# Order and grain of the W1 loads and weight sums beside a masked first layer

## The chip, the cores and the metric

The kernel runs on one core of one Trainium2 chip. The metric is the device time of one execution in microseconds (us), given as the median of several runs. "The profile" is one execution recorded by the hardware profiler; all lines L... are lines of the kernel before unless said otherwise.

## The reference

Eight batches of x (256 rows, 1024 features, float32) go through two residual layers:

```python
sign = (2 * mask - 1).astype(x.dtype)            # one 1024 x 1024 mask per batch
x = x + (einsum('bsi,oi->bso', x, W0) + b0 + einsum('bsi,bio->bso', x, sign) * coeff[:, None, None])
A, Bm = lora_As[itok], lora_Bs[itok]             # rank 16, one of 32 slots per batch
x = x + (einsum('bti,oi->bto', x, W1) + b1 + 2.0 * einsum('btr,bro->bto', einsum('bti,bir->btr', x, A), Bm))
```

In the first layer every batch has a weight matrix of its own, W0 + coeff * (2*mask - 1). In the second all batches share W1, and a small low-rank product is added.

## The kernel before

**First layer.** Work is cut into 64 pieces, numbered k: 8 batches b, two halves h of 512 output features, four groups g of 256 input features (two chunks c of 128). `load(k)` issues on SyncE's queue (SP) the transfers of a piece: the mask block `m` (512 KB), for batch 0 also the block of W0 (512 KB, kept for all batches), for h = 0 the block of x (256 KB). `build(k)` makes the weights: ScalarE (ACT) turns the mask into plus or minus coeff (L188), and VectorE (DVE) adds W0 (L191). TensorE (PE) multiplies in `first_layer` (L215): 8 float32 matmuls a piece, which the trace shows as 16 records. After four pieces VectorE evicts the result with bias and residual into `y` (L229, four instructions). Loads run four pieces ahead of the matmuls in the program and builds two ahead. Masks and built weights have three buffers each (`mpool`, `wpool`): mask k can be loaded only after ScalarE has read mask k-3, and weights k can be built only after TensorE has finished piece k-3.

**Grain.** For k < NG (= 4) the mask and W0 are loaded, and the weights built, by single chunks (two transfers of 256 KB, two ACT and two DVE instructions of 512 columns); from k = 4 on by whole blocks (`chunks`, `load`, `by_chunk`). `by_chunk` reorders the arrays on the host side so that one chunk lies in one stretch of memory.

**Second layer.** Four batches form a group, and there are two groups (pieces 0 to 31 and 32 to 63). After its pieces, `second_layer` multiplies by W1 with a Winograd-Strassen scheme on two levels: seven outer products (A11, A12, S1, S2, S4, S3, A22), each with seven inner leaves (a11, s1, s2, a12, s3, a22, s4). The left leaves are sums of blocks of W1. They are made once, beside the first layer of group 0, by the generator `combine_weights`: W1's 16 blocks (256 KB each, `raw[q, r]`) are loaded, the identity is added on the diagonal (L260), and VectorE forms inner sums (L269 to L275) and outer sums (L286). GpSimd (POOL) writes each leaf to a DRAM scratch (`keep`, L245), from which SyncE loads it when needed (`load_leaves`, L361). The inner sums take their buffers from a pool of seven (`lpool`), which a leaf's write frees.

**Where the W1 loads and the sums stand.** In `load`, each of batch 1's pieces (k = 8 to 15) is followed by two blocks of W1, row by row of the matrix (L176 to L180). `step`, called after each piece as `beside`, takes three items of the sums' generator; the generator is started ahead of b = 1, h = 1, so from k = 12 on. It adds the identity to all four diagonal blocks first and then makes A11, A12, A22, S1, S2, S4, S3. A list scheduler in the framework places the instructions of each engine in order; `tc.issue_after(i)` holds what is under it behind instruction i in that order. [...]

Of the kernel before, what the change touches and what calls it, by code (L numbers as in the profile page):

```python
# [13 lines left out]
P = 128  # L14
OH = 512
CG = 2
OQ = 256
SCALING = 2.0


@with_exitstack
def kernel(
# [36 lines left out]
    nc = tc.nc  # L59
    B, NG, _, _, T = xT.shape  # L60
# [67 lines left out]
    ident = const.tile([P, P], F32, tag="ident", name="ident")  # L128
# [3 lines left out]
    x_sb, m_sb, weff, w0_sb, raw, weff_at = {}, {}, {}, {}, {}, {}  # L132
    pieces = [(b, h, g) for b in range(B) for h in range(2) for g in range(NG)]

    def quad(name):
        return qpool.tile([P, CG, OQ], F32, tag="q", name=name)

    def chunks(k: int):

        return [slice(c, c + 1) for c in range(CG)] if k < NG else [slice(0, CG)]  # L140

    def chunk(a, c: int):

        flat = a.rearrange("p c f -> (p c f)")
        return flat.rearrange("(c p f) -> c p f", c=CG, p=P)[c]

    def load(k: int):


        b, h, g = pieces[k]  # L150
        m_sb[k] = mpool.tile([P, CG, OH], I32, tag="m", name=f"m_{k}")
        if b == 0:
            w0_sb[h, g] = const.tile([P, CG, OH], F32, tag=f"w0{h}{g}", name=f"w0_{h}_{g}")
        if h == 0:
            x_sb[b, g] = xpool.tile([P, CG, T], F32, tag=f"x{g}", name=f"x_{b}_{g}")
        pairs = [(m_sb[k], mask[b, h, g])]
        if b == 0:
            pairs.append((w0_sb[h, g], w0T[h, g]))
        if h == 0:
            pairs.append((x_sb[b, g], xT[b, g]))  # L160
        if k < NG:

            for c in range(CG):
                for i, (t, a) in enumerate(pairs):
                    if i < 2 or k == 0:
                        nc.sync.dma_start(t[:, c], chunk(a, c))  # L166
                    elif c == 0:
                        nc.sync.dma_start(t, a)
        else:
            for t, a in pairs:  # L170
                nc.sync.dma_start(t, a)  # L171
        if k == NG:
            nc.sync.dma_start(b0_sb, b0)
        if k == 2 * NG:
            nc.sync.dma_start(itok_sb, itok)
        if b == 1:  # L176
            n = h * NG + g
            for q, r in ((n // 2, 2 * (n % 2)), (n // 2, 2 * (n % 2) + 1)):
                raw[q, r] = quad(f"w1_{q}_{r}")
                nc.sync.dma_start(raw[q, r], w1T[q, r])  # L180

    def build(k: int):
# [12 lines left out]
    BUILDS_AHEAD = 2  # L195
    n_pieces = len(pieces)
# [4 lines left out]
    def first_layer(b: int, h: int, y, beside):  # L201


        ps = [bank(f"ps1_{b}_{h}_{i}") for i in range(TPH // 2)]
        for g in range(NG):
            k = (b * 2 + h) * NG + g
            if k + LOADS_AHEAD < n_pieces:
                load(k + LOADS_AHEAD)
            if k + BUILDS_AHEAD < n_pieces:
                build(k + BUILDS_AHEAD)  # L210
            w = weff.pop(k)
            for c in range(CG):
                for j in range(TPH):
                    first = g == 0 and c == 0
                    nc.tensor.matmul(  # L215
                        ps[j // 2][:, j % 2, :],
                        lhsT=w[:, c, j * P : (j + 1) * P],
                        rhs=x_sb[b, g][:, c, :],

                        start=first and j % 2 == 0,  # L220
                        stop=g == NG - 1 and c == CG - 1,
                        skip_group_check=True,
                    )
            beside()

        with tc.issue_after(weff_at[k + BUILDS_AHEAD].ins) if b == 0 else nullcontext():
            for j in range(TPH):
                ot = h * TPH + j
                nc.vector.scalar_tensor_tensor(  # L229
                    y[:, j, :],  # L230
                    ps[j // 2][:, j % 2, :],
                    b0_sb[:, ot : ot + 1],
                    x_sb[b, ot // CG][:, ot % CG, :],
                    ALU.add,
                    ALU.add,
                )
# [4 lines left out]
    def keep(outer, inner, t):  # L241
        leaf_at[outer, inner] = dram.tile(
            [P, CG, OQ], F32, tag=f"{outer}{inner}", name=f"leaf_{outer}_{inner}"
        )
        nc.gpsimd.dma_start(leaf_at[outer, inner], t)  # L245

    def combine_weights():


        quads = {  # L250
            f"A{i + 1}{j + 1}": {
                (u, v): raw[2 * i + u, 2 * j + v] for u in range(2) for v in range(2)
            }
            for i in range(2)
            for j in range(2)
        }
        for q in range(NG):
            for c in range(CG):
                d = raw[q, q][:, c, c * P : (c + 1) * P]
                nc.vector.tensor_add(d, d, ident)  # L260
                yield

        def inner(name, blocks, own):
            a11, a12, a21, a22 = (blocks[u, v] for u in range(2) for v in range(2))
            s = {}
            for n in ("s1", "s2", "s3", "s4"):
                s[n] = lpool.tile([P, CG, OQ], F32, tag="l", name=f"{name}_{n}")
                if n == "s1":
                    nc.vector.tensor_add(s[n], a21, a22)  # L269
                elif n == "s2":  # L270
                    nc.vector.tensor_sub(s[n], s["s1"], a11)
                elif n == "s3":
                    nc.vector.tensor_sub(s[n], a11, a21)
                else:
                    nc.vector.tensor_sub(s[n], a12, s["s2"])  # L275
                keep(name, n, s[n])
                yield
            for n, t in (("a11", a11), ("a12", a12), ("a22", a22)):
                if n in own:
                    keep(name, n, t)  # L280

        def outer(name, op, x, y):
            tiles = [tpool.tile([P, 2, CG, OQ], F32, tag="T", name=f"{name}_{u}") for u in range(2)]
            out = {(u, v): tiles[u][:, v] for u in range(2) for v in range(2)}
            for uv in out:
                op(out[uv], x[uv], y[uv])  # L286
                yield
            quads[name] = out

        for i, j, name in ((0, 0, "A11"), (0, 1, "A12"), (1, 1, "A22")):  # L290
            for n, (u, v) in (("a11", (0, 0)), ("a12", (0, 1)), ("a22", (1, 1))):
                leaf_at[name, n] = w1T[2 * i + u, 2 * j + v]
        every = ("a11", "a12", "a22")
        yield from inner("A11", quads["A11"], ("a11", "a22"))
        yield from inner("A12", quads["A12"], ())
        yield from inner("A22", quads["A22"], ("a11", "a22"))
        yield from outer("S1", nc.vector.tensor_add, quads["A21"], quads["A22"])
        yield from inner("S1", quads["S1"], every)
        yield from outer("S2", nc.vector.tensor_sub, quads["S1"], quads["A11"])
        yield from inner("S2", quads["S2"], every)  # L300
        yield from outer("S4", nc.vector.tensor_sub, quads["A12"], quads["S2"])
        yield from inner("S4", quads["S4"], every)
        yield from outer("S3", nc.vector.tensor_sub, quads["A11"], quads["A21"])
        yield from inner("S3", quads["S3"], every)
# [274 lines left out]

    sums = iter(())  # L580

    def step():
        for _ in range(3):
            next(sums, None)

    for group in range(NGROUP):
        if group:
            load_adapters(group)
        y = [
            [  # L590
                ypool.tile([P, TPH, T], F32, tag=f"y{i}{h}", name=f"y_{GB * group + i}_{h}")
                for h in range(2)
            ]
            for i in range(GB)
        ]
        first = Right(f"b11_{group}", [y[0][0], y[1][0]])
        second = Right(f"b21_{group}", [y[0][1], y[1][1]])
        for i in range(GB):
            for h in range(2):
                if i == 1 and h == 1 and group == 0:  # L600
                    sums = combine_weights()
                if i == 3:
                    for _ in (first, second)[h].sums():
                        pass
                first_layer(GB * group + i, h, y[i][h], step)
                if group == 0 and i == 2 and h == 0:
                    late = y[i][h][:, 0, :1]
                    begin_adapters(late)
                    load_adapters(group, late)
        for _ in sums:  # L610
            pass
        second_layer(group, y, first, second)
# [69 lines left out]
```

## Time and profile before

| | us |
|---|---|
| median of 3 runs (lowest to highest) | 424.54 (424.22 to 425.1) |
| the profiled execution | 424.1 |
| its span, first to last instruction | 422.2 |
| TensorE busy in the span | 414.3 (98%) |
| VectorE busy | 271.4 (64%) |
| TensorE's first L215 matmul | 5.83 |
| last stall of TensorE ahead of L215 ends | 61.82 |
| second layer of group 0 begins | 120.80 |

The chain of work that ended last is TensorE alone from 61.82 us to 418.7 us, except for the eviction and the store at the very end. Stretches are given in us from the span's start. A matmul record is drawn with a duration of about 380 ns, but records overlap: TensorE issues one each 216 ns (3.45 us for the 16 records of a piece), so that a stall is read from the distance of starts and not from the busy time.

### The profile page before, as it was taken

To read this page: it belongs to the slowest core of one execution; us is meant where nothing else is said; L and a number is where in the kernel's file an instruction comes from. 1 tells how busy PE (TensorE), PEld (TensorE's weight loads), DVE (VectorE), ACT (ScalarE), POOL (GpSimd) and SP (SyncE) were. 2 spreads that over 40 slices of the span, in tenths; PEclk is the share of its full clock that TensorE was granted. 3 is DMA by queue.
4 is the path that set the end of the run, shared out by engine and by line. 5 is a ranking of instruction groups with operands and counts; after the bars stand their busy time and mean duration, and the time that the engine had idled before them with its cause. 6 is when DMAs were issued, how large, how long until landed. Compare 5 with 4: busy or idle time off the path is not lost.

```text
span 422.2 us, 5655 instructions
## 1 busy us (share of the span) xinstructions
PE 414.3 (98%) x2074; PEld 354.5 (84%) x2074; DVE 271.4 (64%) x395; ACT 110.9 (26%) x126; POOL 38.5 (9%) x77
## 2 busy tenths in 40 slices
PE   8999989999999999999999999999999999999996
PEld 6788868888877888878888888888888688888885
DVE  2457879999765558865735437754573465786693
ACT  4443234333334211011013333333330330101100
POOL 0002313664200000003000000000000000000000
PEclk9999999999999999999999999999999999999999
DMA  8999999999994475557864655744410346654663
GB/s 277 397 404 398 413 408 379 409 336 351 413 395 160 130 254 164 150 174 226 261 222 154 204 201 175 221 152 150 151 50 0 99 108 199 217 153 150 201 205 118
DMA packets 42046, 97.38 MB, mean 231 GB/s; under 512 B 5540, under 2 KB 6308, under 8 KB 42020
## 3 DMA queue, kind: packets, MB, share of 16 engines
q1 hardware_dynamic: 33122, 76.30, 53.7%
q0 software_dynamic: 4288, 12.61, 7.9%
q10 hardware_dynamic: 4610, 8.13, 5.0%
q8 instruction: 16, 0.26, 0.3%
q14 instruction: 10, 0.08, 0.0%
HBM read 77.09 MB, written 19.92 MB: 230 GB/s over the span
## 4 chain that ended last, share of the span: by engine, by line
PE 85%; DMA 12%; SPq 1%; DVE 1%; ACT 0%; issue 0%; DVEq 0%; ACTq 0%
PE ps L215 40%; PE X L378 23%; PE Z L378 12%; DMA w<-w1T 7%; PE Y L378 6%; DMA x<-xT 3%; DMA m<-mask 3%; PE G L395 2%; PE psh L410 2%; SPq L166 1%; ACT w L188 0%; DVE w L191 0%; SPq L171 0%; DVE S L286 0%; DVE c L431 0%
## 5 line engine op out<-in xcount | busy, mean ns | idle before, releaser
L215 PE MATMUL ps<-x,w 128*128 128x256 f32 x1024 | 222.7, 380 | 2.9 <-DVE w L191 2.8
L215 PEld LDWEIGHTS ps<-x,w 128*128 128x128 f32 x1024 | 194.4, 190 | 31.2 <-DVE w L191 4.8
L191 DVE TENSOR_TENSOR w<-w,w 128x1024 f32<-128x1024 f32 (+1 forms) x68 | 78.8, 1159 | 72.5 <-ACT w L188 71.3
L188 ACT ACTIVATE w<-m,neg_c,two_c 128x1024 f32<-128x1024 int32 (+1 forms) x68 | 81.0, 1191 | 163.6 <-PE ps L215 84.2
L512 DVE TENSOR_TENSOR c<-c,e 128x512 f32<-128x512 f32 x48 | 32.0, 687 | 11.2 <-ACT c L404 10.7
L229 DVE SCALAR_TENSOR_TENSOR y<-ps,b_sb,x 128x256 f32<-128x256 f32 x64 | 27.2, 477 | 7.6 <-PE ps L215 7.0
L404 ACT COPY c<-G 128x512 f32<-128x512 f32 x32 | 16.4, 600 | 53.7 <-PE G L395 53.7
L431 DVE TENSOR_TENSOR c<-X,c 128x512 f32<-128x512 f32 (+1 forms) x26 | 16.7, 647 | 16.1 <-PE X L378 16.1
L429 ACT COPY e<-X 128x512 f32<-128x512 f32 x16 | 9.4, 587 | 58.2 <-PE X L378 51.9
L378 PE MATMUL X<-T_t,l_S_s 128*128 128x256 f32 x96 | 22.7, 379 | 0.0
L378 PEld LDWEIGHTS X<-T_t,l_S_s 128*128 128x128 f32 x96 | 18.2, 190 | 2.5
L378 PE MATMUL X<-b_t,l_A_s 128*128 128x256 f32 x64 | 15.5, 386 | 0.0
L431 DVE TENSOR_TENSOR e<-X,e 128x512 f32<-128x512 f32 x16 | 11.0, 686 | 5.8 <-PE X L378 5.8
L378 PEld LDWEIGHTS X<-b_t,l_A_s 128*128 128x128 f32 x64 | 11.8, 190 | 3.0 <-issue 1.5
L431 DVE TENSOR_TENSOR e<-Z,e 128x512 f32<-128x512 f32 x16 | 11.0, 687 | 1.0 <-PE Z L378 0.8
L378 PE MATMUL X<-T,l_S_a 128*128 128x256 f32 x48 | 11.3, 379 | 0.0
L378 PE MATMUL Z<-T_t,l_S_s 128*128 128x256 f32 x48 | 11.3, 379 | 0.0
L378 PE MATMUL Y<-T,l_S_a 128*128 128x256 f32 x48 | 11.3, 379 | 0.0
L378 PE MATMUL X<-T_t,l_S_a 128*128 128x256 f32 x48 | 11.3, 379 | 0.0
L378 PE MATMUL Z<-T,l_S_s 128*128 128x256 f32 x48 | 11.3, 379 | 0.0
L431 DVE TENSOR_TENSOR e<-Y,e 128x512 f32<-128x512 f32 x8 | 5.5, 691 | 7.4 <-PE Y L378 7.4
L378 PEld LDWEIGHTS Y<-T,l_S_a 128*128 128x128 f32 x48 | 9.1, 190 | 1.2
(97 smaller groups left out, 380.0 us busy)
## 6 DMA issues: line engine op xcount, KB each, us to landing
m<-mask SPq DMA_DIRECT2D x60, 512.0 KB, 5.7
l_S_s<-leaf_S_s SPq DMA_DIRECT2D x32, 256.0 KB, 2.7
x<-xT SPq DMA_DIRECT2D x31, 256.0 KB, 6.6
outT<-c ACTq DMA_DIRECT2D x30, 256.0 KB, 3.2
l_A_s<-leaf_A_s SPq DMA_DIRECT2D x24, 256.0 KB, 3.9
l_S_a<-leaf_S_a SPq DMA_DIRECT2D x24, 256.0 KB, 2.6
w<-w1T SPq DMA_DIRECT2D x16, 256.0 KB, 7.6
leaf_S_s<-S_s POOLq DMA_DIRECT2D x16, 256.0 KB, 7.1
```

The costliest lines, as they stand in the source:

```text
L166: nc.sync.dma_start(t[:, c], chunk(a, c))
L188: nc.scalar.activation(w[:, c], m[:, c], AF.Identity, bias=neg_c[:, b : b + 1], scale=two_c[:, b : b + 1])
L191: weff_at[k] = nc.vector.tensor_add(w[:, c], w[:, c], w0_sb[h, g][:, c])
L215: nc.tensor.matmul(ps[j // 2][:, j % 2, :], lhsT=w[:, c, j * P : (j + 1) * P], rhs=x_sb[b, g][:, c, :],  start=first and j % 2 == 0, stop= ...
L229: nc.vector.scalar_tensor_tensor(y[:, j, :], ps[j // 2][:, j % 2, :], b0_sb[:, ot : ot + 1], x_sb[b, ot // CG][:, ot % CG, :], ALU.add, AL ...
L378: nc.tensor.matmul(ps[:, j, :], lhsT=l[:, c, j * P : (j + 1) * P], rhs=r[:, c, :], start=first and c == 0 and j == 0, stop=False, skip_gro ...
L395: nc.tensor.matmul(ps[b][:, j, :], lhsT=lb_pad[rows, o : o + P], rhs=h_sb[rows, :], start=j == 0, stop=j == 1, skip_group_check=True,)
L404: nc.scalar.copy(dest[b // 2][u, b % 2], ps[b])
L410: nc.tensor.matmul(ph[i * S : i * S + R, 0, :], lhsT=a[:, i, c, :], rhs=y[i][c // TPH][:, c % TPH, :], start=(c == 0), stop=(c == NC - 1),)
L429: nc.scalar.copy(out, ps)
L431: nc.vector.tensor_add(out, ps, other)
L512: nc.vector.tensor_add(o, o, x)
```

## The change

Three things change. `BY_CHUNK = 6` takes the place of NG in `chunks`, `load` and `by_chunk`: the six blocks k = 0 to 5 of batch 0 are loaded and built by single chunks, instead of four. The 16 blocks of W1 are loaded in the order A11, A12, A22, A21 (the order in which the sums use them), block n behind the transfers of piece k = 10 + 3n // 4, so one or two a piece over k = 10 to 21, instead of two a piece over k = 8 to 15. The sums start after piece 11, three items a piece up to piece 17 and four from 18 on, and each portion is held behind the weight build of piece k + 2; the identity is added to A11's and A22's diagonal blocks just ahead of their own sums.

```diff
+BY_CHUNK = 6
...
-        return [slice(c, c + 1) for c in range(CG)] if k < NG else [slice(0, CG)]
+        return [slice(c, c + 1) for c in range(CG)] if k < BY_CHUNK else [slice(0, CG)]
...
+    W1_ORDER = [
+        (2 * i + u, 2 * j + v)
+        for i, j in ((0, 0), (0, 1), (1, 1), (1, 0))
+        for u in range(2)
+        for v in range(2)
+    ]
...
-        if k < NG:
+        if k < BY_CHUNK:
 
             for c in range(CG):
                 for i, (t, a) in enumerate(pairs):
...
-        if b == 1:
-            n = h * NG + g
-            for q, r in ((n // 2, 2 * (n % 2)), (n // 2, 2 * (n % 2) + 1)):
+        for n, (q, r) in enumerate(W1_ORDER):
+            if k == 0:
                 raw[q, r] = quad(f"w1_{q}_{r}")
+            if k == 2 * NG + 2 + 3 * n // 4:
                 nc.sync.dma_start(raw[q, r], w1T[q, r])
...
-            beside()
+            beside(k)
...
-        for q in range(NG):
-            for c in range(CG):
-                d = raw[q, q][:, c, c * P : (c + 1) * P]
-                nc.vector.tensor_add(d, d, ident)
-                yield
+
+        def add_identity(blocks):
+            for u in range(2):
+                for c in range(CG):
+                    d = blocks[u, u][:, c, c * P : (c + 1) * P]
+                    nc.vector.tensor_add(d, d, ident)
+                    yield
...
+        yield from add_identity(quads["A11"])
         yield from inner("A11", quads["A11"], ("a11", "a22"))
         yield from inner("A12", quads["A12"], ())
+        yield from add_identity(quads["A22"])
         yield from inner("A22", quads["A22"], ("a11", "a22"))
...
-    def step():
-        for _ in range(3):
-            next(sums, None)
+    def step(k: int):
+
+        nonlocal sums
+        if k == 2 * NG + 3:
+            sums = combine_weights()
+        with tc.issue_after(weff_at[min(k + BUILDS_AHEAD, n_pieces - 1)].ins):
+            for _ in range(3 if k < 4 * NG + 2 else 4):
+                next(sums, None)
...
-                if i == 1 and h == 1 and group == 0:
-                    sums = combine_weights()
...
-    by_chunk(arrays["mask"][0, 0])
-    by_chunk(arrays["w0T"][0])
+    for k in range(BY_CHUNK):
+        by_chunk(arrays["mask"][0, k // NG, k % NG])
+        by_chunk(arrays["w0T"][k // NG, k % NG])
```

## The prediction

> **What bounds the kernel now.** I read the page's busy line and DMA slices first, then who kept TensorE waiting, then the chain of work, then the timeline at the stalls.
>
> ```profile
> PE 414.3 (98%) x2074; PEld 354.5 (84%) x2074; DVE 271.4 (64%) x395; ACT 110.9 (26%) x126; POOL 38.5 (9%) x77
> DMA  8999999999994475557864655744410346654663
> ```
>
> TensorE bounds the span, and the transfers are full only in the first 12 slices: up to about 125 us, the first layer of group 0. A gain must come from TensorE's idle time.
>
> ```profile
> PEld ps L215 <- DVE w L191: 4.8, 5, 1.5
> ```
>
> In the waits of the weight loads, L215 was kept waiting five times, always for the built weights L191. The chain in order of time shows where the last of these ended:
>
> ```profile
> 31.68 6.37 DMA w<-w1T
> 38.07 8.27 DMA w<-w1T
> 46.36 13.55 DMA w<-w1T
> 59.94 0.69 DVE S L286
> 60.63 1.15 DVE w L191
> 61.78 0.04 issue
> 61.82 58.97 PE ps L215 x272
> ```
>
> From 61.82 us on TensorE never waits; what is won or lost before then, or stalled anew later, is the whole effect. The timeline around the stalls:
>
> ```profile
> 5.83 14.67 PE L215 MATMUL ps<-x,w 128*128 128x256 f32 x64
> 21.36 18.83 PE L215 MATMUL ps<-x,w 128*128 128x256 f32 x86 [0.86 <-DVE w L191]
> 47.04 0.69 DVE L275 TENSOR_TENSOR A_s<-w,A_s 128x512 f32<-128x512 f32 x1 [1.49 <-DMA leaf_A_s<-A_s]
> 54.73 1.24 ACT L188 ACTIVATE w<-m,neg_c,two_c 128x1024 f32<-128x1024 int32 x1 [4.71 <-DMA m<-mask]
> 56.00 1.23 DVE L191 TENSOR_TENSOR w<-w,w 128x1024 f32<-128x1024 f32 x1 [2.13 <-ACT w L188]
> 57.28 3.72 PE L215 MATMUL ps<-x,w 128*128 128x256 f32 x16 [1.12 <-DVE w L191]
> 61.82 8.47 PE L215 MATMUL ps<-x,w 128*128 128x256 f32 x38 [0.82 <-DVE w L191]
> 89.17 1.23 DVE L191 TENSOR_TENSOR w<-w,w 128x1024 f32<-128x1024 f32 x1 [0.75 <-ACT w L188]
> ```
>
> By counting records (16 a piece) the stalls lie before pieces 4, 14 and 15. In true starts (x272 records in 58.97 us: 0.216 us each, 3.45 us a piece), piece 4 was 1.02 us late (record 64 starts at 20.12, so piece 4 could start at 20.34), piece 14 was 1.39 late (21.36 + 10 x 3.453 = 55.89 against 57.28), piece 15 1.09 late (60.73 against 61.82). Sum 3.50 us; another 0.70 us hides between the chunks of pieces 0 to 3. The masks of pieces 14 and 15 came late (4.71 us of waiting for one). Last, busy time by stretch:
>
> ```profile
> 40.00:62.00 22.00, 20.06 (x92) 16.99 (x92) 17.40 (x28) 6.24 (x6) 6.47 (x12) 1.00 1.03 409
> 62.00:90.00 28.00, 28.00 (x131) 24.64 (x132) 27.25 (x44) 11.38 (x10) 14.38 (x28) 1.00 1.01 393
> 90.00:112.00 22.00, 22.00 (x104) 19.37 (x102) 21.97 (x32) 8.44 (x7) 11.74 (x22) 1.00 0.99 353
> 112.00:121.00 9.00, 9.00 (x43) 7.94 (x42) 3.12 (x4) 2.48 (x2) 0.00 (x0) 1.00 1.04 411
> ```
>
> The columns after the stretch are its length, then PE, PEld, DVE, ACT, POOL, clock, DMA share, GB/s. VectorE is full from 62 to 112 us (49.2 of 50), yet TensorE doesn't wait there: the second limit, just under the first.
>
> **What the Trainium skill says.** "DMA: Bandwidth & Descriptors", section "Issuing engines are not separate DMA queues": transfers issued by SyncE and GpSimd share the same 16 engines and interleave. The trace agrees: between the arrivals of masks 13 and 14 (48.78 and 54.73) lie 4 units of 256 KB of SyncE, worth 2.6 us at 405 GB/s; the other 3.3 us is about five leaf writes. The same page, "Anatomy of one DMA": a transfer costs about 2 us beside its bytes; the leaf loads land in 2.6 to 2.7 us where the queue isn't full, of which 0.65 are bytes. "VectorE: DVE Perf Modes", section on the TRN2 errata: float32 tensor_tensor takes (N+151)/0.96 ns, 691 ns at N = 512; the trace has 685, but consecutive ones start each 0.60 us, which I use.
>
> **Part 1, pieces 4 and 5 by chunk.** Piece 4's mask and W0 landed at about 18.75 and 20.05; ACT 1.24 and DVE 1.22 followed in series. By halves (0.65 us each) the first is in at 18.75, ACT 0.81 (the chunks' row) runs beside it to 18.9, DVE 0.69 to 19.6: before 20.34. The second half: W0 at 20.05, DVE ends at 20.9, needed at 20.34 + 1.73 = 22.1. So the 1.02 us goes. Next late is piece 7: its DVE add ended at 30.11, set by the mask's arrival (same bytes ahead, so unchanged), and it is now needed at 20.34 + 3 x 3.453 = 30.70: 0.6 us to spare. Two more ACT and two more DVE instructions cost nothing, since both idle there (ACT is busy 7.48 of 20 us).
>
> **Part 2, W1 later.** In units of 256 KB, the arrival of a mask in the trace fits 5.3 + 0.647 x (units queued before it, leaf writes included): mask 14 has 30 units of masks, 16 of W0, 8 of x, 12 of W1, about 10.5 of leaves: 54.8 against 54.73; mask 20 with 104 units 72.6 against 72.75. In the changed order mask 14 has 6 units of W1 ahead and, as A11's first sum now stands behind the build of piece 14 on VectorE, no leaf write: 60 units, 44.1 us. It is needed at 54.87 - 2.7 = 52.2 (1.24 + 1.22 and handing over). Mask 15 is as early. So 1.39 + 1.09 us go. The cover is real, but the bytes return. Three mask buffers stop the prefetch: mask 16 may go out only when ACT has built 13, about 45.95, so the queue idles some 2 us, and later arrivals become 7.5 + 0.647 x units. Mask 24: 97 units of SyncE, 24 leaf writes, 85.8, needed 86.7. Mask 28: 108 + 33 + 2.5 (adapters): 100.3, needed 101.1. Mask 31: 108.8, needed 111.5. Just in time, by under 1 us twice; a miss costs 0 to 1.5 us.
>
> **Part 3, the sums.** They are the same 44 sums and eight identity adds, but the first now runs at about 51 us, not 33, and all must fit in before piece 30. VectorE's list in the changed order from the build of piece 13 to that of 26 has 13 builds (1.14 from start to start), 43 sums (0.60; seven of these are right-hand sums), 16 evictions (0.40), 8 identity adds (0.22) and 3 small copies: 14.8 + 25.8 + 6.4 + 1.8 + 0.2 = 49.0 us. TensorE needs 13 x 3.453 = 44.9. VectorE starts with at most 4.2 us in hand (a build can't start before TensorE leaves piece k-3: 6.9 - 2.7). Waiting for evictions costs about 0.8 more. Walking the list piece by piece, the lead is 3.3 us at piece 20, 0.8 at 22, 0.6 at 24, and piece 26 starts 0.63 us late; by 28 it is 2.9 again. The same walk over the kernel before gives leads of 2.5 to 3.4 us for pieces 18 to 29, as its trace shows, and no stall. An unforeseen wait on VectorE between 75 and 97 us now falls on TensorE one for one. The trace of before has one in that stretch, 0.75 us at 89.17, and none else. I bound the extra by 0 and 2.2 (that and a mask 1.5 late) and take 0.4. A gain from this part is excluded, since no work leaves VectorE.
>
> **Sum.** -3.50 + 0.63 + 0.4 = -2.5 us. The profiled execution (424.1, of which 422.2 is span) would take 421.6; its time is 0.44 under the median 424.54, from which the forecast is 422.0. The second layer has the same work; its leaf loads are issued about 105 us for a start at 118, and group 1 and the last 3.4 us are untouched.
>
> **Rivals.** A, clean: VectorE's list holds, as no stall is seen at a 98% busy VectorE in before: -3.5, 421.0. The walk's 0.63 speaks against. B, half given back: VectorE and the masks of pieces 24 to 31 are both late, 1.6 to 3.2 us: 423.4. For it: margins of 0.8 and 0.9 us in part 2, and only 353 GB/s in 90 to 112 us. C, slower: VectorE waits in order for an `lpool` buffer whose leaf write is queued among full transfers, as at 47.04 (1.49 us). Three such waits after piece 20, where the lead is gone, are 4.5 us: -3.50 + 0.63 + 4.5 = +1.6, 426.2. It decides from 3.5 us of new stalls on. Against it: seven sums after piece 20 span 8 us or more, and writes land in 7 to 8.
>
> **Chances.** Forecast 0.52 (421.5 to 422.9), A 0.22, B 0.18, C 0.08. A measurement can tell about 0.2%, 0.85 us. Faster: forecast, A and a third of B: 0.80. Within: most of B, 0.13. Slower: 0.07. The range leaves out half of A's low side and C: 420.9 to 424.0.
>
> **What would show it.** Part 1: L215 runs on at 20.3 without a gap. Part 2: no gap at pieces 14 and 15, masks 14 and 15 waiting for ACT rather than ACT for them, DMA under full near 45 to 52 us. Part 3: VectorE full from 50 to 108 us and a gap of L215 near 93 to 97 us behind L191. The second layer starts near 118. The forecast is wrong if gaps of L215 after 75 us exceed 2 us, if VectorE waits there for transfers, or if a gap stays before 60 us.

## The result: a small part of the forecast gain

| | before | changed |
|---|---|---|
| median of 14 runs each, us (lowest to highest) | 424.45 (424.03 to 425.1) | 423.74 (423.07 to 425.04) |
| the profiled execution, us | 424.1 | 423.07 |
| its span, us | 422.2 | 421.2 |
| second layer of group 0 begins, us | 120.63 | 119.39 |

The ratio is 0.9985, 95% interval 0.9975 to 0.9994: 0.7 us less, where 2.5 us were forecast. A second measurement of the changed kernel (`e0_again`) gave 0.9994 (0.998 to 1.0007), an interval that holds 1. One execution below, of `e3_sums` (429.48 us), counted as slow and is left out of its median; all others are fast. The beginning of the second layer is read from the timeline of TensorE in both kernels (the chain, which leaves the overlap of records out, has it at 120.80 before).

In the changed kernel L215 is L224, L188 is L197, L191 is L200, L229 is L238, L260 is L271, L269 to L275 are L280 to L286, L286 is L297, L361 is L374 and L378 is L391. First the page's busy line, then the waits of the weight loads:

```profile
PE 414.2 (98%) x2074; PEld 354.3 (84%) x2074; DVE 271.6 (64%) x397; ACT 111.7 (27%) x128; POOL 38.5 (9%) x77
```

```profile
PEld ps L224 <- DVE w L200: 3.8, 6, 1.3
```

The engines do the same work. Weight loads still wait for built weights, 3.8 us instead of 4.8. The chain in order of time (lines picked from it) shows that they wait elsewhere:

```profile
12.19 50.35 PE ps L224 x232
64.21 10.81 DMA w<-w1T
83.29 1.89 DVE S L297 x3
95.81 1.57 DVE y L238 x4
97.38 1.14 DVE w L200
```

TensorE alone carries the chain where before a row of transfers did (to 62 us); then a W1 transfer, sums (L297) and evictions (L238) on VectorE lead up to a build at 97.38. TensorE is free of stalls only from 98.57 us, not from 61.82. Its timeline:

```profile
5.83 3.67 PE L224 MATMUL ps<-x,w 128*128 128x256 f32 x16
10.07 1.97 PE L224 MATMUL ps<-x,w 128*128 128x256 f32 x8 [0.57 <-DMA x<-xT]
12.19 71.06 PE L224 MATMUL ps<-x,w 128*128 128x256 f32 x328 [0.15 <-DVE w L200]
83.43 14.26 PE L224 MATMUL ps<-x,w 128*128 128x256 f32 x64 [0.18 <-DVE w L200]
98.57 20.99 PE L224 MATMUL ps<-x,w 128*128 128x256 f32 x96 [0.88 <-DVE w L200]
```

A row of x328 is drawn without a gap: pieces 1.5 to 21, among them 4, 14 and 15. By true starts (0.216 us a record) the stalls are now 1.18 us before 12.19, and 0.45, 0.2 and 1.12 us before pieces 22 (83.43), 24 (90.51, inside the x64 row) and 26 (98.57). What VectorE did at that time, from its own timeline:

```profile
63.64 0.29 DVE L271 TENSOR_TENSOR w<-w,ident 128x128 f32<-128x128 f32 x1 [1.14 <-DMA w<-w1T]
75.04 0.69 DVE L297 TENSOR_TENSOR S<-w,w 128x512 f32<-128x512 f32 x1 [0.30 <-DMA w<-w1T]
97.30 1.21 DVE L200 TENSOR_TENSOR w<-w,w 128x1024 f32<-128x1024 f32 x1
```

It waited twice for a block of W1, and the build of piece 26 began with no idle time ahead of it: VectorE itself was late. It takes its list in order: of four evictions (L238) that belong together the first ran at 62.03, and the other three ran only at 63.85, behind the identity add that waited 1.14 us. How far VectorE is ahead, its lead, is the time from the end of a piece's build to the start of its matmuls. In this profile it falls from 4.1 us at piece 17 to 3.0 at 18, 2.7 at 20, 1.6 at 21 and 0.06 at 22, 24 and 26. The stretches, with the same columns as before:

```profile
40.00:62.00 22.00, 22.00 (x104) 19.36 (x103) 17.36 (x28) 7.44 (x6) 5.54 (x10) 1.00 0.94 343
62.00:90.00 28.00, 27.82 (x129) 24.18 (x128) 26.56 (x46) 8.70 (x7) 13.23 (x25) 1.00 1.03 410
90.00:112.00 22.00, 21.12 (x97) 18.05 (x96) 22.00 (x33) 8.69 (x7) 13.22 (x26) 1.00 1.01 366
112.00:121.00 9.00, 9.00 (x43) 7.92 (x43) 7.27 (x10) 2.48 (x2) 1.28 (x3) 1.00 1.03 412
```

TensorE's 1.94 us of idle time between 40 and 62 us are gone, 1.06 us come back between 62 and 112 us, and VectorE now has more left to do in the last stretch (7.27 us busy instead of 3.12), among it right-hand sums of the second layer (L382) and an eviction. From 40 to 62 us the transfers fell from 409 to 343 GB/s.

The books of the two profiled executions, in us: stalls before pieces 4, 14 and 15, -3.50; among the first pieces, 0.70 to 1.18, +0.48; before pieces 22, 24 and 26, +1.77. The sum is -1.25, and the second layer begins 1.24 sooner. The span is 1.0 shorter; the other 0.2 lies in the second layer, and its cause is open. The changed kernel's profiled execution is the quickest of its 14 runs, 0.67 us under their median. Which stall makes up that 0.67 no trace shows; the second profile, below, has 0.5 us more before piece 22, but it too is of an execution 0.9 us under its median.

### The profile page after: what moved, and what is told of

It reads as the page before. It is cut to its first block, busy times and chain, and to the rows that moved or that the text cites. A ratio compares the mean times of both kernels' runs of the same rounds, so it can differ in the third digit from the quotient of the medians.

```text
span 421.2 us, 5669 instructions
## 1 busy us (share of the span) xinstructions
PE 414.2 (98%) x2074; PEld 354.3 (84%) x2074; DVE 271.6 (64%) x397; ACT 111.7 (27%) x128; POOL 38.5 (9%) x77
## 2 busy tenths in 40 slices
DMA packets 42622, 97.38 MB, mean 231 GB/s; under 512 B 5604, under 2 KB 6372, under 8 KB 42596
## 4 chain that ended last, share of the span: by engine, by line
PE 88%; DVE 5%; DMA 4%; issue 1%; SPq 1%; ACT 0%; DVEq 0%
PE ps L224 43%; PE X L391 23%; PE Z L391 12%; PE Y L391 6%; DMA w<-w1T 3%; PE G L408 2%; PE psh L423 2%; DMA m<-mask 1%; DVE S L297 1%; DVE w L200 1%; SPq L175 1%; DVE y L238 1%; ACT w L197 0%; DVE S_s L280 0%; DVE S_s L282 0%
## 5 line engine op out<-in xcount | busy, mean ns | idle before, releaser
L224 PE MATMUL ps<-x,w 128*128 128x256 f32 x1024 | 222.6, 380 | 1.8 <-DVE w L200 1.2
L224 PEld LDWEIGHTS ps<-x,w 128*128 128x128 f32 x1024 | 194.2, 190 | 30.1 <-DVE w L200 3.8
L197 ACT ACTIVATE w<-m,neg_c,two_c 128x1024 f32<-128x1024 int32 (+1 forms) x70 | 81.7, 1167 | 162.1 <-PE ps L224 95.7
L200 DVE TENSOR_TENSOR w<-w,w 128x1024 f32<-128x1024 f32 (+1 forms) x70 | 79.1, 1131 | 69.7 <-ACT w L197 67.8
L238 DVE SCALAR_TENSOR_TENSOR y<-ps,b_sb,x 128x256 f32<-128x256 f32 x64 | 27.4, 478 | 7.7 <-PE ps L224 7.0
L391 PE MATMUL X<-T_t,l_S_s 128*128 128x256 f32 x96 | 22.7, 379 | 0.0
L391 PEld LDWEIGHTS X<-T_t,l_S_s 128*128 128x128 f32 x96 | 18.2, 190 | 2.5
L391 PE MATMUL X<-b_t,l_A_s 128*128 128x256 f32 x64 | 15.5, 386 | 0.0
L391 PEld LDWEIGHTS X<-b_t,l_A_s 128*128 128x128 f32 x64 | 11.8, 190 | 3.0 <-issue 1.5
L391 PE MATMUL X<-T,l_S_a 128*128 128x256 f32 x48 | 11.3, 379 | 0.0
L391 PE MATMUL Y<-T,l_S_a 128*128 128x256 f32 x48 | 11.3, 379 | 0.0
L391 PE MATMUL X<-T_t,l_S_a 128*128 128x256 f32 x48 | 11.3, 379 | 0.0
L391 PE MATMUL Z<-T_t,l_S_s 128*128 128x256 f32 x48 | 11.3, 379 | 0.0
L391 PE MATMUL Z<-T,l_S_s 128*128 128x256 f32 x48 | 11.3, 379 | 0.0
L382 DVE TENSOR_TENSOR T<-y,T 128x1024 f32<-128x1024 f32 x8 | 9.8, 1219 | 0.8 <-DMA leaf_S_a<-S 0.7
```

What stands on the lines that cost most here:

```text
L197: nc.scalar.activation(w[:, c], m[:, c], AF.Identity, bias=neg_c[:, b : b + 1], scale=two_c[:, b : b + 1])
L200: weff_at[k] = nc.vector.tensor_add(w[:, c], w[:, c], w0_sb[h, g][:, c])
L224: nc.tensor.matmul(ps[j // 2][:, j % 2, :], lhsT=w[:, c, j * P : (j + 1) * P], rhs=x_sb[b, g][:, c, :],  start=first and j % 2 == 0, stop= ...
L238: nc.vector.scalar_tensor_tensor(y[:, j, :], ps[j // 2][:, j % 2, :], b0_sb[:, ot : ot + 1], x_sb[b, ot // CG][:, ot % CG, :], ALU.add, AL ...
L382: nc.vector.tensor_sub(t, x[v], y[v])
L391: nc.tensor.matmul(ps[:, j, :], lhsT=l[:, c, j * P : (j + 1) * P], rhs=r[:, c, :], start=first and c == 0 and j == 0, stop=False, skip_gro ...
```

## The experiments

The theory, T, is that the first two parts gain what was forecast and the third costs about twice its price, because the sums, begun late and in portions held behind builds, leave VectorE no lead. The rivals: R1, the start of the first pieces costs the gain; R2, transfers (W1 or leaf writes) come late to VectorE's list; P, the portion of four items from k = 18 on puts the builds behind. All ratios are against the kernel before on the same chip.

### The change taken again, and in three parts

`e0_again` is the changed kernel without an edit.

> The changed kernel once more, beside the other runs on the same chip. Theory T (what was won ahead of piece 16 is given back on VectorE: 0.6 us because its list is too full, 1.0 us because it waits in order for W1 blocks that now land late): no gap before pieces 4, 14 and 15, gaps of 1.5 to 2.5 us in all before pieces 22 to 26, gain of 0.5 to 1.2 us. Rival R1 (the gain is lost in the first three pieces, whose start differs from run to run): the gap ahead of piece 2 is 1 us or more and the gaps at 22 to 26 under 1 us. Rival R2 (transfers that were put off come back as masks that are late): ACT waits for masks just ahead of each late build, and VectorE idles before it.

`e1_chunks` is the kernel before with the first part alone:

```diff
+BY_CHUNK = 6
...
-        return [slice(c, c + 1) for c in range(CG)] if k < NG else [slice(0, CG)]
+        return [slice(c, c + 1) for c in range(CG)] if k < BY_CHUNK else [slice(0, CG)]
...
-        if k < NG:
+        if k < BY_CHUNK:
```

> The kernel before with the six blocks by single chunks alone. The prediction's step: the 1.02 us at piece 4 goes, 1.0 us faster. Theory T now adds that masks 14 and 15 arrive when the transfers let them, whatever TensorE does: piece 4 starts 1 us earlier, but the gap before piece 14 grows by the same 1 us, and the time stays within 0.3 us of the kernel before. A rival that holds the first pieces' start for the cause sees a gain or loss in that start alone.

`e2_loads` is the second part alone (W1 later, the identity in the new order), four blocks by chunk, sums begun and portioned as before:

```diff
-BY_CHUNK = 6
+BY_CHUNK = 4
...
-        if k == 2 * NG + 3:
-            sums = combine_weights()
-        with tc.issue_after(weff_at[min(k + BUILDS_AHEAD, n_pieces - 1)].ins):
-            for _ in range(3 if k < 4 * NG + 2 else 4):
-                next(sums, None)
+        for _ in range(3):
+            next(sums, None)
...
+                if i == 1 and h == 1 and group == 0:
+                    sums = combine_weights()
```

> W1's later loads in the new order and the identity adds beside their own sums, but the sums begin and are portioned as before (from piece 12, three a piece, not held behind a build), and four blocks by chunk. Theory T: the gaps at 14 and 15 are gone (six units fewer ahead of mask 14, 3.9 us), the gap at piece 4 stays; if VectorE's portions are no larger than before it keeps its lead, and what is left is its waiting for W1: 1.0 to 2.5 us faster than before, with waits of VectorE for W1 of 1 us or more. R2: gaps after piece 20 remain with VectorE idle.

`e3_sums` is the third part alone (sums as changed, W1 loaded as before, four blocks by chunk):

```diff
-BY_CHUNK = 6
+BY_CHUNK = 4
...
-        for n, (q, r) in enumerate(W1_ORDER):
...
-            if k == 2 * NG + 2 + 3 * n // 4:
+        if b == 1:
+            n = h * NG + g
+            for q, r in ((n // 2, 2 * (n % 2)), (n // 2, 2 * (n % 2) + 1)):
```

> The sums begun and portioned as in the change, but W1 loaded as before (two blocks behind each of pieces 8 to 15, row by row), and four blocks by chunk. Theory T: no leaf write stands ahead of mask 14 any more, so the gaps at 14 and 15 are gone; W1 is all in by 50 us, so VectorE never waits for it and the gap before piece 26 is the full list's alone, 0.1 to 0.6 us: 1.5 to 2.5 us faster than before. R2 (late transfers, not W1 waits, make the late gaps): gaps of 1.5 us or more after piece 20 as in the changed kernel, 0.5 to 1 us faster.

Measured:

| kernel | median us | ratio (95%) |
|---|---|---|
| changed, again | 424.11 | 0.9994 (0.998 to 1.0007) |
| `e1_chunks`: chunks alone | 425.30 | 1.0018 (1.0009 to 1.0028) |
| `e2_loads`: loads alone | 423.62 | 0.9975 (0.9964 to 0.9986) |
| `e3_sums`: sums alone | 423.57 | 0.9974 (0.9961 to 0.9988) |

The changed kernel's second profile has the pattern of the first, a little larger. TensorE's timeline:

```profile
83.54 14.26 PE L224 MATMUL ps<-x,w 128*128 128x256 f32 x64 [0.67 <-DVE w L200]
```

In true starts this stall, before piece 22, is 0.94 us. With 0.2 at piece 24 and 1.15 at piece 26 these are 2.27 us. VectorE waited 2.0 us for W1, once, and 0.9 us for a leaf write to free an `lpool` buffer.

Chunks alone make the kernel slower, by 0.76 us, which I had not expected. Its trace, TensorE's timeline (L216 is its matmul line):

```profile
28.83 20.99 PE L216 MATMUL ps<-x,w 128*128 128x256 f32 x96 [0.78 <-DVE w L192]
50.39 7.17 PE L216 MATMUL ps<-x,w 128*128 128x256 f32 x32 [0.56 <-DVE w L192]
58.60 3.72 PE L216 MATMUL ps<-x,w 128*128 128x256 f32 x16 [1.03 <-DVE w L192]
62.84 58.97 PE L216 MATMUL ps<-x,w 128*128 128x256 f32 x272 [0.53 <-DVE w L192]
```

The gap before piece 4 is gone, but 1.05 us are lost before piece 6 and 0.83 before piece 12, and 14 and 15 stall for 2.1 us together (2.5 before). At 12, 14 and 15 ScalarE waits for the masks: with a full queue and W1 still ahead of the masks, a mask comes when the queue brings it, whenever TensorE is ready. At piece 6 it is not the mask, which ScalarE takes at 24.94 us here and at 24.92 in the changed kernel, where no gap follows. VectorE waits for the block of W0:

```profile
27.55 1.23 DVE L192 TENSOR_TENSOR w<-w,w 128x1024 f32<-128x1024 f32 x1 [1.53 <-DMA w<-w0T]
```

Of the nine profiles with six blocks by chunk only this one and that of `e8_no_hold` (1.66 us) have this wait; why, no run shows. The chunks also cost something. In this profile ScalarE reaches the eighth chunk 0.64 us later than before, but it is as late in `e2_loads`, with four blocks by chunk (17.43 us here, 17.53 there). And between the ACT of the eighth chunk and that of mask 6 lie 7.51 us, 7.54 in both profiles of the changed kernel, against 7.21 before and 7.24 in `e2_loads` (all with the same bytes in between): 0.3 us. The second layer begins 1.0 us later than before; how much of the loss of 0.76 in the medians is the 0.3, the block of W0 or the start, no run here tells apart.

Loads alone take away the gaps at pieces 14 and 15 and leave 0.2 us at piece 29; the gap before piece 4 stays (1.1 us). The second layer begins at 119.15 but then waits 1.83 us for its first inner leaf. The sums alone gain less than T expected (1.1 us, not 1.5 to 2.5). The profiled execution of `e3_sums` is the slowest of its 23; its trace is read below for rival C alone. So the loads alone bring 1.1 us and the sums alone bring 1.1 us, and the two together, next, bring nothing.

### Loads and sums together, and the chunks beside each

`e4_four` is the changed kernel with four blocks by chunk (loads and sums, no part 1). `e5_loads_six` is `e2_loads` with six (chunks and loads, sums as before).

```diff
-BY_CHUNK = 6
+BY_CHUNK = 4
```

> The changed kernel with four blocks by chunk, as before (W1's loads and the sums as changed). The prediction's own step: without part 1 it is 1.0 us slower than the changed kernel. Theory T: W1's blocks land at the times of the transfers' queue, not of TensorE, and VectorE waits for them; with pieces 1 us later these waits shrink by as much, so the time is that of the changed kernel within 0.4 us, 0.3 us better at most for the 0.3 us that the chunked transfers cost in the queue.

> W1's later loads, six blocks by chunk, but the sums begun at piece 12 and portioned as before (three a piece, not held behind a build). Theory T: no gap at 4, 14, 15, and none at 22 to 26, since VectorE's list keeps a lead of about 3 us there; VectorE may wait 1 to 2 us for W1 within that lead: 1.5 to 2.5 us faster than the kernel before, about 1 us faster than the changed one. If instead late masks or the start make the loss, it stays at the changed kernel's time.

Measured: `e4_four` 424.77 us, 1.0005 (0.9996 to 1.0014); `e5_loads_six` 421.77 us, 0.9941 (0.9926 to 0.9956). In the trace of `e5_loads_six` TensorE loses 0.2 us in all between 8.07 us and the second layer, which begins at 117.20, and waits once after that, 0.89 us for a leaf.

This decides the main question. The same chunks and the same late W1 loads, with the sums begun at k = 12 in threes and not held, take 0.44 to 0.53% less than the changed kernel (0.9941 against 0.9985 and 0.9994): the changed order of the sums costs 1.9 to 2.3 us. VectorE waits as long for W1 there, 1.4 + 0.4 us, and TensorE doesn't notice, as VectorE has a lead (2.3 to 2.6 us at pieces 22 to 28).

In `e4_four`, against my expectation, removing part 1 costs only 0.5 to 0.8 us (0.0011 to 0.0020 in ratio). Its trace has 1.1 us before piece 4 and 2.15 before 22, 24 and 26. I had argued that a TensorE that is 1 us later needs less lead. It does not: masks are released by TensorE's pace, the W1 blocks stand behind masks in the queue, and so W1 is later too (VectorE's first wait for it ends at 65.16 us, not 63.64); VectorE waits 1.3 + 0.2 us all the same.

### What makes the held sums late: work, W1 or the hold

`e6_six_off` takes work from VectorE: six of the inner sums of S1 and S2 are left out, and ScalarE copies stand in their place.

```diff
-                if n == "s1":
+                if name in ("S1", "S2") and n != "s1":
+                    nc.scalar.copy(s[n], s["s1"])
+                elif n == "s1":
```

> The changed kernel with six of VectorE's sums (the second to fourth inner sums of S1 and S2) replaced by copies on ScalarE of the first, so that these leaves hold wrong values; buffers, transfers and their sizes are the same. It frees VectorE of 3.6 us before piece 26. Theory T (the list is full): the gaps at 22 to 26 vanish though the W1 waits stay, 1.5 to 2.2 us faster than the changed kernel. R2 (transfers put off come back): gaps stay at 1.5 us or more, the same time as the changed kernel within 0.4 us.

`e7_w1_early` has the blocks of W1 two pieces sooner (k = 8 to 19), the sums as changed.

```diff
-            if k == 2 * NG + 2 + 3 * n // 4:
+            if k == 2 * NG + 3 * n // 4:
```

> The changed kernel with every W1 block loaded two pieces sooner (pieces 8 to 19, not 10 to 21). Theory T: VectorE no longer waits for W1 (1.4 to 2.0 us in the changed kernel's traces), masks 14 and 15 keep several us to spare, and the late gaps fall from about 2 us to the 0.6 to 0.9 us of the full list: 0.8 to 1.4 us faster than the changed kernel. If the list alone makes the gaps, the time stays within 0.3 us of the changed kernel.

Measured: `e6_six_off` 423.05 us, 0.9966 (0.9954 to 0.9979); `e7_w1_early` 422.19 us, 0.9957 (0.994 to 0.9973). Six sums are 3.6 us of VectorE; without them the kernel is 0.8 to 1.2 us faster than the changed one, less than T's 1.5 to 2.2. Of the stalls one of 0.7 us is left at piece 26, and a new one of 0.4 stands at piece 30. VectorE waits 1.4 us for W1, 1.7 us for leaf writes (the copies keep their turn in `lpool`), and 1.57 us ahead of the build of piece 24, whose mask landed at 86.61: with the list relieved, a late mask is what counts there, as R2 says. With W1 sooner, VectorE waits for no W1 block and no leaf write, and TensorE's timeline reads:

```profile
5.84 90.88 PE L224 MATMUL ps<-x,w 128*128 128x256 f32 x416
97.59 20.99 PE L224 MATMUL ps<-x,w 128*128 128x256 f32 x96 [0.88 <-DVE w L200]
```

The gap at piece 22 is gone, 0.1 us is left at 24, and the one at 26 stays at 1.1 us. That is not the full list alone, for VectorE waits for other things:

```profile
47.43 1.35 DVE L238 SCALAR_TENSOR_TENSOR y<-ps,b_sb,x 128x256 f32<-128x256 f32 x3 [2.60 <-PE ps L224]
71.73 1.22 DVE L200 TENSOR_TENSOR w<-w,w 128x1024 f32<-128x1024 f32 x1 [0.97 <-ACT w L197]
```

The evictions at 47.43 stand ahead of the build of piece 13, which so begins with a lead of 1.6 us and not of 4.2; and the build of piece 20 waits for ScalarE, which had mask 20 only at 70.46 (70.73 in the changed kernel, where VectorE came later still). No run has the held sums with none of these waits. The 1.1 us at piece 26 are the same in all four profiles that hold portions of four and lose time there (the changed kernel twice, `e4_four`, `e7_w1_early`): piece 24 starts without a lead in each, and from its build to that of piece 26 VectorE needs 8.06 us where TensorE needs 6.9.

In the medians the earlier W1 is worth 1.2 to 1.6 us. `e3_sums` and `e4_four`, which differ in W1's loads alone, say the same: 1.3 us (0.9974 and 1.0005).

### Without the hold, with portions of three, and the best of both

`e8_no_hold` lets the list scheduler place the sums; `e9_three` keeps the hold and takes three items throughout; `e10_both` is `e5_loads_six` with the edit of `e7_w1_early`.

```diff
-        with tc.issue_after(weff_at[min(k + BUILDS_AHEAD, n_pieces - 1)].ins):
-            for _ in range(3 if k < 4 * NG + 2 else 4):
-                next(sums, None)
+        for _ in range(3 if k < 4 * NG + 2 else 4):
+            next(sums, None)
```

> The changed kernel without the hold: the sums still begin after piece 11, three a piece and four from piece 18, but no longer stand behind the build of piece k + 2. VectorE's list then has A11's first sum ahead of the build of piece 13 instead of behind that of 14, and the walk over it gives a lead of 1.8 us at piece 26 where the changed kernel's gives -0.6. Theory T (the sums are put off too far, and the hold does it): gaps at 22 to 26 of 0 to 0.5 us, 1.2 to 2.2 us faster than the changed kernel. Rival P (the portion of four makes the list too full): at most 0.5 us faster than the changed kernel.

```diff
-            for _ in range(3 if k < 4 * NG + 2 else 4):
+            for _ in range(3):
```

> The changed kernel with three items a piece all through, the hold kept. The walk over VectorE's list gives a lead of 1.8 us at piece 26 here too. Rival P: the gaps at 22 to 26 go, 1.2 to 2.2 us faster than the changed kernel. Theory T in its narrow form (the hold alone) expects at most 0.5 us. If both this and the run without the hold gain, what counts is the sum of the list ahead of piece 26, and either of the two relieves it.

> W1 two pieces sooner (pieces 8 to 19) together with the sums begun and portioned as before and six blocks by chunk: both reliefs at once. Theory T: the kernel with the old sums alone has no gap of TensorE left behind piece 2, so nothing more is to be had: the same time within 0.4 us, 421.4 to 422.2. The walk warns of a lead of only 0.9 us at piece 13, as VectorE waits there for the eviction of batch 1, with a loss of up to 0.5 us. If W1's waits still cost where they don't show in a profile, it gains 0.5 us or more.

Measured: `e8_no_hold` 422.57 us, 0.9939 (0.992 to 0.9959); `e9_three` 423.81 us, 0.9984 (0.9975 to 0.9993); `e10_both` 421.75 us, 0.9929 (0.991 to 0.9948).

Without the hold there is no gap at pieces 22 to 26, though VectorE waits 2.1 us for W1 and the portions are still of four: it has the lead to absorb them. (Its profile loses 1.2 us at piece 6, where the block of W0 is late as in `e1_chunks`, and 0.56 at piece 30 instead; the loss at piece 6 itself adds to VectorE's lead. In ratio the kernel is 2.0 to 2.3 us faster than the changed one, as much as `e5_loads_six`.) With three a piece the gaps at 22 to 26 go as well, and the second layer begins at 118.12, 1.3 us sooner. But the time is that of the changed kernel. TensorE's timeline shows why:

```profile
121.68 1.99 PE L391 MATMUL Z<-b_t,l_A_s 128*128 128x256 f32 x8 [1.67 <-DMA l_A_s<-leaf_A_s]
```

The leaves of the second layer are loaded into the seven buffers of `lpool`, and this load takes the buffer of an inner sum of S4. That sum's write is issued at 102.81, not 100.20, and the leaf load at 112.57, not 109.99; it lands at 121.63, where TensorE could have used it at 119.85. The loss moved from the first layer into the second. So P is right on the gaps and wrong on the time: held sums must hurry or be missed later. `e10_both` is no better than `e5_loads_six` within the intervals, as expected; these two and `e8_no_hold` are the best versions of this study. `e10_both` differs from `e7_w1_early` in the sums alone and is 1.2 us faster (0.9929 and 0.9957): with W1 sooner, too, the changed sums cost something.

## Why the prediction was wrong

**Part 1, half right.** The 1.02 us before piece 4 went. "Two more ACT and two more DVE instructions cost nothing" left out the other side, the transfers: from the eighth chunk to mask 6 they take 0.3 us more. The prediction took piece 7 for the next that could be late; in `e1_chunks` it was piece 6, through its block of W0. The first pieces lost 0.48 us more than before in this profile. Whether any of that is the change is open: with four blocks by chunk, as before, they lose 0.7 us in the profile of before but 1.35 in `e2_loads` and 1.5 in `e4_four`; with six, 0.8 (`e5_loads_six`) to 2.2 (`e10_both`). Alone, part 1 makes the kernel slower by 0.76 us, beside part 2 it gains 1.4 us (0.9975 to 0.9941), and in the changed kernel 0.5 to 0.8: a stall removed early is a gain only if nothing after it comes at a time of its own.

**Part 2, right in its gain.** Pieces 14 and 15 no longer stall, ACT waits there for TensorE and not for a mask, and no build between 60 and 117 us waited for ACT. But the masks were in time only because VectorE was late: mask 24 came at 87.74 against 85.8 forecast, and its build started at 89.24 with ACT done at 88.98. Where an experiment took work or waits from VectorE, a mask was what it waited for next (1.57 us in `e6_six_off`, 0.97 in `e7_w1_early`). The idle stretch of the queue was forecast and mis-sized. Between 42 and 53 us the transfers moved

```profile
42.00:53.00 11.00, 11.00 (x53) 9.68 (x52) 7.60 (x14) 4.36 (x4) 1.27 (x3) 1.00 0.85 279
```

279 GB/s against the 413 of a full slice, so (413 - 279) / 413 x 11 = 3.6 us were idle, not 2. `e7_w1_early` fills it (357 GB/s). The arrival of masks was worked out with care and the arrival of the W1 blocks not at all: they are the ones that were late. The block for the wait at 63.64 was issued at 54.38 and took 9.2 us, beside masks and leaf writes.

**Part 3, the step that failed: the extra wait.** The price of the sums was 0.63 us for the full list and 0.4 for an unforeseen wait; the profiles have 1.77 and 2.27 us of stalls, the medians 1.9 to 2.3 (`e5_loads_six` against the changed kernel). The mechanism was the one named: VectorE's list without a lead, a gap at piece 26, and a wait on VectorE that "falls on TensorE one for one". The term that was too small is the 0.4. From the build of piece 13 (46.58 us) to that of piece 26 (97.30) VectorE executes in 50.72 us just the 83 instructions that the prediction counted: 49.1 us of list, where 49.0 were forecast, 1.44 of waiting for W1, and 0.18 of other idle time. Without stalls TensorE, which began piece 13 at 52.01, would have begun piece 26 at 96.90; it did at 98.57, 1.67 us late. Less the 1.44 this leaves 0.2, so the 0.63 was not too small; of the 0.8 for waiting for evictions hardly any came. In the second profile piece 26 is 2.17 us late, and VectorE waited 2.03 us for W1. So the extra, taken at 0.4 from a wait for ScalarE at 89.17, was 1.4 to 2.0 of waits for W1. The trace of before has such a wait, at a sum in the prediction's own chain, just ahead of the late build of piece 15:

```profile
59.94 0.69 DVE L286 TENSOR_TENSOR S<-w,w 128x512 f32<-128x512 f32 x1 [0.91 <-DMA w<-w1T]
```

The prediction passed over it, and the change loads the blocks later still. My bounds, 0 to 2.2, held. What the list costs when W1 is in time stays open: 1.67 less 1.44 says 0.2 us, `e7_w1_early` has 1.3 in stalls with other waits in them, and its median lies 1.2 us above that of `e10_both`.

**The sum.** -3.50 + 0.63 + 0.4 should have been -3.50 + 1.77 + 0.48 = -1.25 for the profile. For the medians the books also close: `e5_loads_six`, with the same loads and chunks and without the cost of the sums, gains 2.5 to 2.9 us, about what is left of 3.50 after 0.89 us of waiting for a leaf in the second layer; less 1.9 to 2.3 this gives the changed kernel's small gain.

**The rivals.** B was the right one in time (423.4 forecast) and in size of stalls (1.6 to 3.2). Of its two causes VectorE's lateness held, through W1's blocks; the masks were late as it says, but in the changed kernel behind a later VectorE. A's argument, that a VectorE busy at 98% did not stall before, fails on the lead: 2.5 to 3.6 us at pieces 18 to 29 before, 0.06 at 22, 24 and 26 after. C's mechanism appears, 0.9 us in the second profile and 1.3 in `e4_four`, after piece 26, where the lead is back and TensorE doesn't stall. In the profiled execution of `e3_sums`, 5.9 us above their median, one such wait is long:

```profile
112.25 0.69 DVE L286 TENSOR_TENSOR S_s<-S,S_s 128x512 f32<-128x512 f32 x1 [3.78 <-DMA leaf_S_s<-S_s]
```

TensorE then stands idle for 4.50 us before piece 30. So one such wait can be enough. How often it comes, and why this leaf write was so late, a single execution doesn't say.

## What to carry to other kernels

Work that hides beside a bound engine, on an engine that is itself full, is paid from the lead which that engine has; before moving such work later, walk its list for the lead at each point, and walk the arrival of every operand in it, not only of those that were late before. A hold that keeps side work from delaying the main work also keeps it from using idle time early; here, with W1 loaded late, leaving it out made the kernel 2.0 to 2.3 us faster (`e8_no_hold`). When one wait is taken away, look for the next one just behind it: here mask 24 was ready only 0.3 us before the late VectorE came to it. Judge the parts of a change in combination: here parts worth -1.1 and -1.1 gave nothing together, and one worth +0.8 alone gave -1.4 beside the right partner.

## What the runs showed of the hardware

On the same saturated queue, from 15 to 20 us, the transfers moved 381 to 385 GB/s in the nine profiles with six blocks by chunk and 395 to 398 in three with four (before, `e2_loads`, `e4_four`). The size of a transfer alone is not the reason: from 10 to 15 us all these kernels load single chunks (256 KB, each partition's row 2 KB; whole blocks have 512 KB and rows of 4 KB), and 11 of the 12 profiles show 390 to 398 GB/s there. What sets the lower rate is open. A 256 KB transfer, 0.65 us of bytes, took 9.2 us from issue to landing among masks and leaf writes. And in the profiled execution of `e3_sums`, where TensorE stood idle for 4.50 us up to 116.72, the granted clock is 1.00 from 105 to 110 us, 0.50 from 115 to 120 and 0.87 from 120 to 125.
